# Graph attention over 400 000 edges: the row gathers of a pair of sections issued in four groups of two, four to five pairs ahead, in place of two groups of four, two to three pairs ahead

## The chip, the cores and the metric

The kernel runs on one core of a Trainium2 chip. The metric is the device time of one execution in microseconds (us), and smaller is better. Engines are named as in the profile: PE is TensorE (matrix products and transposes), DVE is VectorE, ACT is ScalarE, POOL is GpSimd, SP is SyncE. PEld is the loading of PE's weights, which overlaps its matmuls.

## The reference, cut to what matters

There are N = 12500 nodes with C = 128 channels and E = 400000 edges, sorted by target node. Each edge has 32 attributes and one weight; H = 8 heads.

```python
h = relu(layernorm(x))
msg_src, msg_dst = h @ w_src + b_src, h @ w_dst
rad = silu(silu(edge_attr_32 @ w1 + b1) @ w2 + b2) @ w3 + b3      # 32 -> 64 -> 64 -> 128
message = (msg_src[src] + msg_dst[dst]) * edge_weight1 * rad
message = message @ w_sep + b_sep                                 # 128 -> 256
alpha, value = per head, 16 + 16: smooth_leaky_relu(first), second
score = sum(alpha * alpha_dot)                                    # E x 8
att = softmax of score over the edges of one target node
out = x + segment_sum(value * att, dst) @ w_proj + b_proj
```

The row `msg_src[src]` is wanted for every edge, in a random order: these are the gathers of this case.

## The kernel before, in words

A first stage computes the two node tables `t_src` and `t_dst` in device memory (up to about 115 us in the profile). A last stage, from about 5610 us on, finishes the nodes. Between them stands `windows()`, nearly all of the time, and the change lies in it.

`windows()` works on pairs: a pair is 1000 edges, that is 2 sections of 500, and a section is 4 tiles of T = 125 edges. There are NP = 400 pairs. A function `step(k)` issues work for several pairs at once. The order of the instructions on each engine is the order in which `step` writes them down (the scheduler is switched off here); every engine runs its own list in order and waits for semaphores of the others. One step on PE, with the line of the profile in parentheses and c = k - 12:

1. `mlp3(k)` (L795): third layer of the radial network for pair k, 2 matmuls. Behind it DVE makes `rad` (L799), the layer's result plus bias, times the edge weights.
2. `sources(k,1)` (L808): 4 transposes of gathered rows of section 1 into the PSUM tile `pm1`.
3. `message(k)` (L816): 6 small matmuls that add the targets' rows through one-hot matrices. Behind it DVE makes `mT` (L821), that is (pm + bias) times `rad`, in two halves.
4. `values(c,0)` (L908): 4 matmuls for an older pair; DVE makes `pvx` (L910) of them.
5. `alphas(k,0)` (L825): needs the first half of mT. ACT makes `sl` (L827), DVE `al` (L829).
6. `mlp1(k+2)` (L763).
7. `values(c,1)` (L908), then on DVE `one_hot(c)` (L895, L898).
8. `sources(k+1,0)` (L808): 4 transposes of section 0 of the next pair into `pm0`.
9. `alphas(k,1)` (L825).
10. `mlp2(k+1)` (L778); ACT makes `h`, which the next step's mlp3 reads.
11. `sums(c)` (L919): 8 accumulating pairs of matmuls, copied out by ACT (`ob`, L923).
12. One step in eight: the transposes of the softmax (L880). Another one in eight makes indices for the gathers (`prep_make`, L697 and L700).
13. `e_T(k+3)` (L754): transposes of attributes; ACT copies them (`eT`, L756).
14. In odd steps: `scores(k)` (L836) for pairs k-1 and k; ACT copies them (`Sp`, L839).

The PSUM tiles have one buffer each, and together they fill its 8 banks: `p3` (two, shared by the three layers), `m1`, `pm0`, `pm1`, `pa`, `V` and `misc`, which is shared by sums, scores and the softmax.

The gathers (L744) are indirect DMAs issued by POOL: 128 rows of 512 bytes each, one per tile, so eight in a step. `gather(k,f)` fills a tile of 4 x 128 elements per partition, named gs0 or gs1, with two buffers of each name. It stands directly behind the `sources` call that frees the buffer it will fill, and POOL has nothing else to do in the steps: `gather(k+2,1)` waits for the transposes of `sources(k,1)`, `gather(k+3,0)` for those of `sources(k+1,0)`. POOL so issues two groups of four in each step.

The loads of attributes are issued by ACT, and the targets' rows (`md`, L724) are loaded four pairs ahead.

Of the kernel before, what the change touches and what calls it, by code (L numbers as in the profile page):

```python
# [21 lines left out]
F32 = mybir.dt.float32  # L22
# [8 lines left out]
P = 128  # L31
C = 128
# [13 lines left out]
T = 125  # L46
TS = 4
SEC = T * TS
# [8 lines left out]
def gnn_kernel(ctx: ExitStack, tc: tile.TileContext, a: dict, out: bass.AP):  # L57
    nc = tc.nc
# [46 lines left out]
    ident = const.tile([P, P], F32, name="ident")  # L105
# [22 lines left out]
    def zero(i):  # L128

        av = agg[0:N, :].rearrange("(p t) c -> p (t c)", p=RP)  # L130
        nc.sync.dma_start(out=av[:, i * zc * ROW:(i + 1) * zc * ROW], in_=z)
        if i == 0:
            nc.sync.dma_start(out=agg[N:N + W, :], in_=z[:W, 0:ROW])
# [527 lines left out]
    def windows():  # L661
# [5 lines left out]
        with tc.tile_pool(name="wk2", bufs=2) as sp, tc.tile_pool(name="ps", bufs=1, space=PSUM) as pp, \  # L667
                tc.manual_schedule(), ExitStack() as held:
            lp = held.enter_context(tc.tile_pool(name="ld", bufs=2))
            prep, e_g, d_g, w_g, md, gath = {}, {}, {}, {}, {}, {}  # L670
            eTs, h1s, h2s, ohT, m3, mr, mTs, als, S_all, sms, Ps, Pem, pvx, ohs, accs, xs, Ms, pms = (
                {} for _ in range(18))


            def prep_load(u):
                t0 = u * P
                ri = lp.tile([P, 2, T], I32, name="ri")
                rb = lp.tile([P, 1], I32, name="rb")
                nc.sync.dma_start(out=ri[:, 0, :], in_=src_t[t0:t0 + P, :])
                nc.sync.dma_start(out=ri[:, 1, :], in_=dst_t[t0:t0 + P, :])  # L680
                at = dst_t[t0:t0 + P, 0:1]
                (step, _), *_ = at.ap
                at = bass.AP(at.tensor, at.offset, [[step * TS, P // TS], [0, TS], [1, 1]])
                with nc.allow_non_contiguous_dma(reason="a word per tile"):
                    nc.sync.dma_start(out=rb, in_=at)
                prep[u] = (ri, rb)
# [22 lines left out]
            def load_d(g):  # L709
                d_g[g] = lp.tile([P, 2, SEC], I32, name="d_b")  # L710
                for f in range(2):
                    nc.sync.dma_start(
                        out=d_g[g][f * W:(f + 1) * W],
                        in_=dst_p[f:f + 1, 2 * g:2 * g + 2, :].to_broadcast([W, 2, SEC]))

            def load_w(k):
                w_g[k] = lp.tile([P, PR], F32, name="w_b", bufs=4)
                nc.sync.dma_start(out=w_g[k], in_=ew_p[:, k, :].to_broadcast([P, PR]))

            def load_md(k):  # L720
                md[k] = lp.tile([P, C], F32, name="md", bufs=5)
                at = [nc.sync.value_load(base[0:1, f, k:k + 1]) for f in range(2)]
                for f in range(2):
                    nc.sync.dma_start(out=md[k][f * W:(f + 1) * W, :], in_=t_dst[ds(at[f], W), :])  # L724
# [11 lines left out]
                else:  # L736
                    nc.vector.tensor_sub(m3[k][:, 2, :], mr.pop(k), m3[k][:, 1, :])

            def gather(k, f):
                gs = lp.tile([P, TS, C], F32, name=f"gs{f}", bufs=2)  # L740
                idx, _ = prep[k // 16]
                for j in range(TS):
                    t = k % 16 * 8 + f * TS + j
                    nc.gpsimd.indirect_dma_start(  # L744
                        out=gs[:, j, :], out_offset=None, in_=t_src[:, :],
                        in_offset=bass.IndirectOffsetOnAxis(ap=idx[:, t:t + 1], axis=0))
                gath[k, f] = gs


            def e_T(k):  # L750
# [49 lines left out]
                                                   op0=ALU.add, op1=ALU.mult)  # L800
                return rad

            def sources(k, f):

                gs = gath.pop((k, f))
                pms[k, f] = pp.tile([C, SEC], F32, name=f"pm{f}")
                for t in range(TS):
                    nc.tensor.matmul(pms[k, f][:, t * T:(t + 1) * T], gs[:T, t, :], ident[:T, :T],  # L808
                                     start=(t == 0), stop=False, is_transpose=True, skip_group_check=True)

            def message(k, rad):
# [11 lines left out]
            def alphas(k, f):  # L823
                pa = pp.tile([C, SEC], F32, name="pa")
                nc.tensor.matmul(pa, w_a, mTs[k][:, f * SEC:(f + 1) * SEC], start=True, stop=True)  # L825
                sl = sp.tile([C, SEC], F32, name="sl")
                nc.scalar.activation(sl, pa, AF.Silu, bias=b_a, scale=1.0)  # L827
                al = sp.tile([C, SEC], F32, name="al", bufs=6)
                nc.vector.scalar_tensor_tensor(al, pa, 0.25, sl, op0=ALU.mult, op1=ALU.add)  # L829
                als[2 * k + f] = al  # L830
# [46 lines left out]
            def softmax_T(m):  # L877
                pt = pp.tile([T, TS, P], F32, name="misc")
                for t in range(TS):
                    nc.tensor.transpose(pt[:, t, :], Ps[m][:, t * T:(t + 1) * T], ident)  # L880
                Pem[m] = sp.tile([T, TS, MQ, H], F32, name="Pem")
                nc.scalar.copy(Pem[m].rearrange("p t q h -> p t (q h)"), pt)
# [43 lines left out]
            def store_win(c):  # L926
                nc.sync.dma_start(out=win[c * P:(c + 1) * P, :], in_=accs[c])

            def store(c, f):
                at = nc.sync.value_load(base[0:1, f, c:c + 1])  # L930
                nc.sync.dma_start(out=agg[ds(at, W - 1), :], in_=accs[c][f * W:(f + 1) * W - 1, :])
# [16 lines left out]
            def has(k):  # L948
                return 0 <= k < NP
# [5 lines left out]
            def step(k):  # L955
                c = k - LAG
                if has(c - 1):
                    store_win(c - 1)
                    store(c - 1, 0)

                if k % 16 == 4 and has(k + 12):
                    prep_load((k + 12) // 16)
                if has(k + 3):
                    load_w(k + 3)
                if has(k + 4):
                    load_md(k + 4)
                if k % 2 and has(k + 3):
                    load_d((k + 3) // 2)
                if has(k + 4) and (k + 4) % MP == 0:
                    load_sm((k + 4) // MP)  # L970
                if has(c - 1):
                    store(c - 1, 1)
                if 0 <= 2 * k < NZ:
                    for i in range(2 * k, min(2 * k + 2, NZ)):
                        zero(i)
                if k % 16 == 8 and has(k + 8):
                    prep_make((k + 8) // 16)
                i, q = divmod(k - 40, MP)
                if 0 <= i < Q and q == 0:
                    load_x(i)  # L980
                if 0 <= i < Q and q == 7:
                    add_x(i)
                if has(k + 1):
                    split_md(k + 1, 0)
                if has(c):
                    weights(c)
                rad = mlp3(k) if has(k) else None
                if has(k):
                    sources(k, 1)
                if has(k + 2):  # L990
                    gather(k + 2, 1)
                if has(k):
                    message(k, rad)
                if has(c):
                    values(c, 0)
                if has(k + 1):
                    split_md(k + 1, 1)
                if has(k):
                    alphas(k, 0)
                if has(k + 6) and k >= -4:  # L1000
                    load_e(k + 6)
                if has(k + 1):
                    split_md(k + 1, 2)
                if has(k + 2):
                    mlp1(k + 2)
                if has(c):
                    values(c, 1)
                    one_hot(c)

                if has(k + 1):  # L1010
                    sources(k + 1, 0)
                if has(k + 3):
                    gather(k + 3, 0)
                if has(k):
                    alphas(k, 1)
                if has(k + 1):
                    mlp2(k + 1)
                    one_hot_T(k + 1)
                    split_md(k + 1, 3)
                if has(c):  # L1020
                    sums(c)
                m, r = divmod(k, MP)
                if has(k - MP):
                    if r == 1:
                        softmax_up(m - 1)
                    elif r == 2:
                        softmax_down(m - 1)
                        softmax_exp(m - 1)
                    elif r == 3:
                        softmax_T(m - 1)  # L1030
                if has(k + 3):
                    e_T(k + 3)
                if has(k) and k % 2 == 1:
                    scores(k)
# [187 lines left out]
    with tc.tile_pool(name="fin", bufs=3) as fp, tc.tile_pool(name="fin1", bufs=1) as f1, \  # L1222
# [7 lines left out]
        gs, qs, qTs, has = {}, {}, {}, {}  # L1230
# [104 lines left out]
```

## Time and profile before

| quantity | value |
|---|---|
| median of 3 runs (lowest, highest) | 5814.39 us (5809.36, 5816.74) |
| the profiled execution | 5814.39 us, its span 5812.6 us |
| mean granted clock of PE | 0.903 of full speed |
| mlp3 of the first and the last pair | 128 us and 5604 us, so 13.7 us a step |
| PE busy from 128 to 5603 us | 4402 us of 5475 us |
| POOL busy from 128 to 5603 us | 3105 us |
| a gather on POOL | 973 ns mean, 3200 of them |
| a transpose of gathered rows on PE | 300 ns mean, pipelined; 553.9 us busy in all |

How to read what follows: a group is all instructions of one line, engine and form; its columns are busy time, mean duration of one in ns, and idle time of its engine just before it with what ended that. A line of the waits says which engine and line waited for what, with the total in us, how often, and the longest. In the timeline each row has start, length, engine, line, and in brackets the idle time before it and its releaser. A window's row has its length, the busy time of PE, PEld, DVE, ACT and POOL with instructions, then the granted clock, the DMA engines' share and GB/s.

### The profile page before, as it was taken

To read this page: it belongs to the slowest core of one execution; us is meant where nothing else is said; L and a number is where in the kernel's file an instruction comes from. 1 tells how busy PE (TensorE), PEld (TensorE's weight loads), DVE (VectorE), ACT (ScalarE), POOL (GpSimd) and SP (SyncE) were. 2 spreads that over 40 slices of the span, in tenths; PEclk is the share of its full clock that TensorE was granted. 3 is DMA by queue.
4 is the path that set the end of the run, shared out by engine and by line. 5 is a ranking of instruction groups with operands and counts; after the bars stand their busy time and mean duration, and the time that the engine had idled before them with its cause. 6 is when DMAs were issued, how large, how long until landed. Compare 5 with 4: busy or idle time off the path is not lost.

```text
span 5812.6 us, 87691 instructions
## 1 busy us (share of the span) xinstructions
PE 4590.1 (79%) x29692; PEld 2537.5 (44%) x29692; DVE 3082.3 (53%) x6005; ACT 1903.7 (33%) x4595; POOL 3127.7 (54%) x3223
## 2 busy tenths in 40 slices
PE   5688788877788888888888888788888877788874
PEld 3244444444444444444444444444444444444444
DVE  5355555555555555555555555555555555555556
ACT  4233333333333333333333333333333333333321
POOL 1555555555555555555555555555555555555520
PEclk8898999989988989999899998998988999999987
DMA  6555555555555555555555555555555555555533
GB/s 200 162 138 129 136 139 137 141 132 141 136 132 135 144 131 138 146 134 136 143 133 140 143 130 133 139 132 130 137 129 135 139 127 128 133 134 133 137 82 144
DMA packets 901335, 794.74 MB, mean 137 GB/s; under 512 B 530270, under 2 KB 776974, under 8 KB 900746
## 3 DMA queue, kind: packets, MB, share of 16 engines
q1 hardware_dynamic: 394664, 520.94, 30.1%
q0 software_dynamic: 102816, 210.37, 17.1%
q10 hardware_dynamic: 403394, 57.74, 6.6%
q8 instruction: 234, 3.83, 0.3%
q14 instruction: 227, 1.86, 0.1%
HBM read 648.39 MB, written 140.67 MB: 136 GB/s over the span
## 4 chain that ended last, share of the span: by engine, by line
PE 70%; DVE 9%; issue 9%; another core or an unknown queue 6%; ACT 4%; DMA 2%; SPq 0%; ACTq 0%; DVEq 0%
PE pa L825 13%; PE V L908 13%; PE misc L919 8%; PE p L795 7%; PE pm L808 7%; PE pm L816 6%; PE p L763 4%; PE misc L836 4%; PE p L778 4%; PE m L754 3%; DVE mT L821 3%; DVE rad L799 2%; DVE pvx L910 1%; PE misc L880 1%
## 5 line engine op out<-in xcount | busy, mean ns | idle before, releaser
L744 POOL DMA_INDIRECT gs<-t_src,idx x3200 | 3113.2, 973 | 2470.6 <-PE pm L808 988.1
L827 ACT ACTIVATE sl<-pa,c_b_a 128x500 f32<-128x500 f32 x800 | 541.8, 677 | 2307.1 <-PE pa L825 1075.3
L825 PE MATMUL pa<-mT,c_w_a 128*128 128x500 f32 x1600 | 899.6, 646 | 389.4 <-DVE mT L821 305.1
L799 DVE SCALAR_TENSOR_TENSOR rad<-p,c_fc_b,w_b 128x500 f32<-128x500 f32 x800 | 553.4, 733 | 1145.9 <-PE p L795 541.4
L908 PE MATMUL V<-c_w_v,mT 128*125 128x128 f32 x6208 | 984.6, 307 | 125.0 <-DVE pvx L910 89.8
L908 PEld LDWEIGHTS V<-c_w_v,mT 128*125 128x125 f32 x6208 | 826.4, 207 | 441.8 <-issue 316.4
L910 DVE TENSOR_TENSOR pvx<-V,Pem 125x512 f32<-125x512 f32 x776 | 532.8, 687 | 680.6 <-PE pa L825 275.6
L829 DVE SCALAR_TENSOR_TENSOR al<-pa,sl 128x500 f32<-128x500 f32 x800 | 541.7, 677 | 553.8 <-ACT sl L827 335.7
L919 PE MATMUL misc<-pvx,oh 125*64 125x136 f32 x6400 | 486.4, 297 | 263.8 <-DVE oh L898 135.9
L821 DVE SCALAR_TENSOR_TENSOR mT<-pm,c_b_src,rad 128x500 f32<-128x500 f32 x800 | 554.3, 732 | 115.6 <-PE V L908 38.1
L919 PEld LDWEIGHTS misc<-pvx,oh 125*64 125x64 f32 x6400 | 380.9, 143 | 439.6 <-issue 278.0
L808 PE MATMUL pm<-ident,gs 125*128 125x125 f32 x3200 | 553.9, 300 | 3.3 <-DMA gs<-t_src,idx 2.4
L808 PEld LDWEIGHTS pm<-ident,gs 125*128 125x128 f32 x3200 | 400.4, 155 | 339.7 <-issue 335.1
L795 PE MATMUL p<-h,w3b 64*128 64x500 f32 x1600 | 487.6, 689 | 13.9 <-ACT h L781 7.7
L825 PEld LDWEIGHTS pa<-mT,c_w_a 128*128 128x128 f32 x1600 | 257.6, 202 | 455.8 <-DVE mT L821 350.5
L836 PE MATMUL misc<-al,w_s 128*32 128x500 f32 x1600 | 241.3, 669 | 168.8 <-issue 83.3
L923 ACT COPY ob<-misc 128x136 f32<-128x136 f32 x400 | 109.1, 273 | 707.8 <-PE m L754 400.7
L816 PE MATMUL pm<-ohT,m 64*128 64x500 bf16 x2400 | 338.6, 390 | 0.0
L763 PE MATMUL p<-eT,w1b 64*128 64x250 f32 x1600 | 307.9, 465 | 3.1 <-ACT eT L756 3.1
L778 PE MATMUL p<-h,w2b 64*64 64x250 f32 x3200 | 278.6, 420 | 26.1 <-ACT h L766 23.5
L766 ACT ACTIVATE h<-p,b 128x500 f32<-128x500 f32 x400 | 273.0, 683 | 38.3 <-issue 12.0
L781 ACT ACTIVATE h<-p,b 128x500 f32<-128x500 f32 x400 | 269.4, 673 | 30.6 <-remote 14.0
(145 smaller groups left out, 3274.6 us busy)
## 6 DMA issues: line engine op xcount, KB each, us to landing
w_b<-in_edge_weight SPq DMA_DIRECT2D x400, 500.0 KB
d_b<-in_dst SPq DMA_DIRECT2D x400, 250.0 KB
gs<-t_src,idx POOLq DMA_INDIRECT x3200
e_t<-in_edge_attr ACTq DMA_DIRECT2D x400, 125.0 KB
sc_d<-Sp SPq DMA_DIRECT2D x200, 250.0 KB
win<-ob SPq DMA_DIRECT2D x400, 68.0 KB
agg<-ob SPq DMA_DIRECT2D x800, 33.5 KB
md<-t_dst SPq DMA_DIRECT2D x800, 32.0 KB
```

The lines of the kernel that those rows point to most:

```text
L744: nc.gpsimd.indirect_dma_start(out=gs[:, j, :], out_offset=None, in_=t_src[:, :], in_offset=bass.IndirectOffsetOnAxis(ap=idx[:, t:t + 1], ...
L795: nc.tensor.matmul(p3[:, f, 0:SEC], w3b[s, :], h2s[k][s, :], start=True, stop=True)
L799: nc.vector.scalar_tensor_tensor(rad[:, s], p3[:, f, 0:SEC], b3, w_g[k][:, s], op0=ALU.add, op1=ALU.mult)
L808: nc.tensor.matmul(pms[k, f][:, t * T:(t + 1) * T], gs[:T, t, :], ident[:T, :T], start=(t == 0), stop=False, is_transpose=True, skip_group ...
L816: nc.tensor.matmul(pm[f], m3[k][s, j, :], ohT[k][s, :], start=False, stop=(j == 2), skip_group_check=True)
L821: nc.vector.scalar_tensor_tensor(mTs[k][:, s], pm[f], b_n, rad[:, s], op0=ALU.add, op1=ALU.mult)
L825: nc.tensor.matmul(pa, w_a, mTs[k][:, f * SEC:(f + 1) * SEC], start=True, stop=True)
L827: nc.scalar.activation(sl, pa, AF.Silu, bias=b_a, scale=1.0)
L829: nc.vector.scalar_tensor_tensor(al, pa, 0.25, sl, op0=ALU.mult, op1=ALU.add)
L908: nc.tensor.matmul(V[:, t, :], mTs[c][:, o:o + T], w_v, start=True, stop=True)
L910: nc.vector.tensor_mul(pvx[c][:, f, :, 0:C].rearrange("p t (h k) -> p t h k", h=H), V.rearrange("p t (h k) -> p t h k", h=H), Pem[c // MP] ...
L919: nc.tensor.matmul(acc[f * W:(f + 1) * W, :], ohs[c][:, f * TS + t, :], pvx[c][:, f, t, :], start=(t == 0), stop=(t == TS - 1), skip_group ...
```

## The change

The gathers of a section are split in two halves. `gather(k,f,h)` and `sources(k,f,h)` handle two tiles each; the tiles in SBUF become four names of 2 x 128 elements per partition with four buffers each, so that they take twice the room. Each gather still stands right behind the transposes that free its buffer, but fetches for four to five pairs ahead. The four groups of two transposes are put at four places of the step: behind mlp3, behind `values(c,1)`, behind `alphas(k,1)`, and ahead of `e_T`. So two of the transposes of section 1 that stood behind mlp3(k) are done at the end of step k-1. All other instructions of PE, and the lists of DVE, ACT and SP, keep their order; POOL's first gather of each of the four groups waits for PE.

The description of the change also names the loads of attributes by ACT and the rows of targets four pairs ahead; those are in the kernel before already, and the diff has only this:

```diff
-            def gather(k, f):
-                gs = lp.tile([P, TS, C], F32, name=f"gs{f}", bufs=2)
+            def gather(k, f, h):
+                gs = lp.tile([P, TS // 2, C], F32, name=f"gs{f}{h}", bufs=4)
                 idx, _ = prep[k // 16]
-                for j in range(TS):
-                    t = k % 16 * 8 + f * TS + j
+                for j in range(TS // 2):
+                    t = k % 16 * 8 + f * TS + h * 2 + j
                     nc.gpsimd.indirect_dma_start(
...
-                gath[k, f] = gs
+                gath[k, f, h] = gs
...
-            def sources(k, f):
-
-                gs = gath.pop((k, f))
-                pms[k, f] = pp.tile([C, SEC], F32, name=f"pm{f}")
-                for t in range(TS):
-                    nc.tensor.matmul(pms[k, f][:, t * T:(t + 1) * T], gs[:T, t, :], ident[:T, :T],
+            def sources(k, f, h):
+
+                gs = gath.pop((k, f, h))
+                if h == 0:
+                    pms[k, f] = pp.tile([C, SEC], F32, name=f"pm{f}")
+                for j in range(2):
+                    t = 2 * h + j
+                    nc.tensor.matmul(pms[k, f][:, t * T:(t + 1) * T], gs[:T, j, :], ident[:T, :T],
                                      start=(t == 0), stop=False, is_transpose=True, skip_group_check=True)
...
                 rad = mlp3(k) if has(k) else None
                 if has(k):
-                    sources(k, 1)
-                if has(k + 2):
-                    gather(k + 2, 1)
+                    sources(k, 1, 1)
+                if has(k + 4):
+                    gather(k + 4, 1, 1)
...
                 if has(k + 1):
-                    sources(k + 1, 0)
-                if has(k + 3):
-                    gather(k + 3, 0)
+                    sources(k + 1, 0, 0)
+                if has(k + 5):
+                    gather(k + 5, 0, 0)
                 if has(k):
                     alphas(k, 1)
+                if has(k + 1):
+                    sources(k + 1, 0, 1)
+                if has(k + 5):
+                    gather(k + 5, 0, 1)
                 if has(k + 1):
                     mlp2(k + 1)
...
+                if has(k + 1):
+                    sources(k + 1, 1, 0)
+                if has(k + 5):
+                    gather(k + 5, 1, 0)
                 if has(k + 3):
                     e_T(k + 3)
```

## The prediction

> **What bounds the kernel now.** I read the page first, then the groups of instructions, the waits, the windows of two steps and the timeline of the same two.
>
> From the page:
>
> ```profile
> PE 4590.1 (79%) x29692; PEld 2537.5 (44%) x29692; DVE 3082.3 (53%) x6005; ACT 1903.7 (33%) x4595; POOL 3127.7 (54%) x3223
> PE 70%; DVE 9%; issue 9%; another core or an unknown queue 6%; ACT 4%; DMA 2%; SPq 0%; ACTq 0%; DVEq 0%
> L744 POOL DMA_INDIRECT gs<-t_src,idx x3200 | 3113.2, 973 | 2470.6 <-PE pm L808 988.1
> L808 PE MATMUL pm<-ident,gs 125*128 125x125 f32 x3200 | 553.9, 300 | 3.3 <-DMA gs<-t_src,idx 2.4
> ```
>
> PE carries the end. The transposes wait 2.4 us for gathered rows in the whole run, so fetching rows earlier (the deeper look-ahead) can bring nothing by itself. POOL has room: eight gathers a step take about 10 us of a step of 13.7 us (the 400 steps stand between 128 and 5604 us).
>
> The waits of PE in the steps:
>
> ```profile
> PE pa L825 <- DVE mT L821: 305.1, 216, 4.7
> PE misc L919 <- DVE oh L898: 135.9, 94, 8.8
> PE misc L919 <- issue: 121.2, 128, 2.0
> PE misc L836 <- issue: 83.3, 66, 2.5
> PE misc L836 <- ACT ob L923: 66.4, 58, 5.3
> ```
>
> The first line is `alphas(k,0)` waiting for the DVE chain mlp3, rad, mT; the next two are `sums`. The windows of one odd and one even step (length first; ahead of the DMA share, the granted clock) show that the odd one is stalled and partly at a lower clock:
>
> ```profile
> 3002.40:3018.30 15.90, 12.21 (x78) 6.85 (x76) 8.69 (x17) 4.41 (x12) 10.51 (x11) 0.89 0.62 163
> 3018.30:3029.00 10.70, 9.42 (x72) 5.33 (x68) 7.01 (x14) 3.80 (x9) 6.33 (x7) 1.00 0.51 145
> ```
>
> Their timeline (start, length) says why:
>
> ```profile
> 3001.21 0.94 POOL L744 DMA_INDIRECT gs<-t_src,idx  x1 [1.29 <-PE p L778]
> 3002.49 1.11 PE L795 MATMUL p<-h,w3b 64*128 64x500 f32 x4
> 3004.95 0.95 POOL L744 DMA_INDIRECT gs<-t_src,idx  x1 [0.30 <-issue]
> 3005.60 1.38 DVE L799 SCALAR_TENSOR_TENSOR rad<-p,c_fc_b,w_b 128x500 f32<-128x500 f32 x2 [2.50 <-PE pm L816]
> 3008.01 1.10 PE L825 MATMUL pa<-mT,c_w_a 128*128 128x500 f32 x2 [2.02 <-DVE mT L821]
> 3010.09 2.07 PE L908 MATMUL V<-c_w_v,mT 128*125 128x128 f32 x8
> ...
> 3018.38 1.11 PE L795 MATMUL p<-h,w3b 64*128 64x500 f32 x4
> 3019.54 1.38 DVE L799 SCALAR_TENSOR_TENSOR rad<-p,c_fc_b,w_b 128x500 f32<-128x500 f32 x2 [2.65 <-PE p L795]
> 3021.71 1.03 PE L825 MATMUL pa<-mT,c_w_a 128*128 128x500 f32 x2
> ```
>
> In the even step rad starts 0.05 us after mlp3 has ended (3018.38 + 1.11 = 3019.49). In the odd one it starts 2.00 us after (3003.60 to 3005.60), though DVE idles 2.5 us and the rest of its data has long been there. Its start coincides with mlp3's semaphore update in the trace: PE had finished, its update came late. I set every PE update against the end of its matmul. They come 0.014 us after it, except while gathers run back to back. A run of four lasts 4.77 us; from 3.5 us after its start until about 1 us after its end, 9 of 10 updates are held, by 1.0 to 1.9 us (medians). In the 72 runs of eight, lags stay mostly under 1 us up to 5.2 us after the start, and are 2.7 to 3.4 us from 5.5 to 11.9 us. In the shown odd step the run of four began at 3001.21, so mlp3's end falls into its tail: rad is late, pa waits 2.02 us, and the next values matmuls run at half clock (2.07 us, where unstalled ones take 1.14). In even steps the other end of the same thing holds the update of `values(c,1)`: DVE's pvx and one_hot come late and `sums` waits. So the gathers' pattern in time sets about half of PE's idle time, though POOL is on no chain. That these held updates come from the gathers is read from their coincidence.
>
> The Trainium skill speaks against this reading: "SBUF — State Buffer", "Who interferes with whom", says that DMA traffic never contends with a compute engine and that PE waits for nobody's port. By it only the order on PE would count, and the sum would be +34 us; the rows above show the holds in this trace, whatever carries them.
>
> **The change part by part.** Sums are made against the profiled execution, 5814.39 us, the median of the three runs (span 5812.6, 1.8 around it).
>
> *Work.* Gathers, transposes and bytes stay 3200, 3200 and equal: 0. The buffers double in SBUF: 0. POOL waits for PE four times a step in place of two; what is queued behind each such wait are gathers only, and their rows are wanted four to five steps later: 0 as a wait.
>
> *Order on PE.* Two of the four transposes that stood between mlp3 and message go ahead of e_T and the next mlp3. Four take 0.58 us (mlp3's end to message's start less the 0.03 between), two 0.27 us net. At the end of an odd step they fill the wait of scores L836 (83.3 + 66.4 us over 200), and in the following even step pa was reached at +3.33 us, when mT's first half is done (0.05 + 1.11 + 1.38 + 0.73 = +3.27): 0. At the end of an even step nothing covers them, mlp3 starts 0.27 us later, and behind it the odd step is bound by the chain over rad: +0.27 x 200 = +54 us. `alphas(k,1)` moves ahead of two transposes: its results come 0.27 us sooner for scores, at most -54 us; I take -20, as scores' waits are 150 us and only some are for it.
>
> *When the gathers run.* Each group starts at the transposes that free its buffer. From the order and the durations of an unstalled step these are, from mlp3's start: 6.3 us (sources(k+1,0,0)), 7.3 (only alphas stands between), 9.2 (after sums), and the next step's, about 1.45 us after its mlp3. That is no quarter of a step each. One gather with its gap is 1.25 us, a group 2.5. Asked at 6.3, 7.3 and 9.2, three groups run back to back, 6.3 to 13.8; with steps of 10.7 to 13.7 us the fourth is asked for at 12.2 to 15.2, and follows with a gap of at most 1.4 us. So runs of six to eight, once a step, take the place of fours twice a step. By the rows of runs of eight, updates would be held from 5.5 us after the start, 11.8, to about 1 us after the end, 14.8 to 17.3: that is around mlp3 and message of the *next* step, in every step and not in every second.
> - Even steps: mlp3's update becomes late. Bounds: 0 (flushed just before) and 2.0 us as in odd steps; I take the middle, as the shown odd step is at the tail of its run and here the place is not sure to a microsecond: +1.0 x 200 = +200 us.
> - The lower clock behind such a wait: between 0 and 1.2 us (values 0.93, transposes 0.26); for a wait of half the size I take a quarter: +0.3 x 200 = +60.
> - Odd steps, held already: 2.0 us could become 2.7 to 3.4 (runs of eight), so 0 to +1.4; I take 0.5, the low side, as part lies behind the message's matmuls: +100.
> - `values(c,1)` ends at 6.2 us, ahead of the run: its hold goes. Bounds 0 and the whole of the two waits of sums, -257 us; I take -150, as pvx then waits for the later mT and al on DVE.
>
> Sum: 54 - 20 + 200 + 60 + 100 - 150 = +244 us, **6058 us**. What is late next is rad in every step. The terms' ends give -311 (0 for the order and the late updates, -54, -257) and +974 (54 + 400 + 240 + 280), so 5503 to 6788.
>
> **Rivals.**
> 1. *Faster: short bursts are not held.* In the runs of four the first two gathers mostly see no lag (median 0.02 to 0.04 us), and after a pause of more than 2.2 us the count begins anew. If the groups really come apart, by stalls that spread their triggers, the holds go: pa's 305 and sums' 257 us, and about 150 us of lower clock, 712 in all. That decides from a pause of some 1.4 us after each group on. Against it: the triggers at 6.3 and 7.3 stand 1.0 us apart in any step. Half of it, 356 us, gives 5458.
> 2. *Only the order counts:* the holds neither grow nor shrink, as both patterns keep POOL busy equally long. +34, 5848 us, slower. For it: POOL's 3113 us do not change.
> 3. *The full hold in every step:* 2.0 us and the clock in even steps, 1.4 more in odd ones, nothing back from sums beyond half: 974 - 128 = +846, 6660 us. For it: the 2.7 to 3.4 us of runs of eight. Against it: a stalled step is longer, so the run ends earlier in the next one and frees mlp3's update again.
>
> The change failing to do what it says (a quarter of a step apart) is in the forecast itself.
>
> **How the numbers follow.** Forecast 0.45, rival 1 0.27, rival 2 0.13, rival 3 0.15. A measurement of this kernel tells about 0.2%, 12 us, from no change. Rival 1 is faster, a small part of the forecast's low side as well: 0.28; within 0.2%: 0.04; slower 0.68. The forecast's own range is 5800 to 6350. For 8 in 10 it reaches down into rival 1, to 5480, and up into rival 3, to 6500.
>
> **What would show it.** Right: in the timeline, POOL runs of six or more gathers a step; rad starting 1 us and more after mlp3's end in even steps too; pa's wait for mT well over 305 us in twice as many instances; sums' waits below 257. Wrong: gathers in pairs with gaps over a microsecond, pa's wait falling below 150 us and a granted clock over 0.93 (rival 1); or the same waits as now with runs of another length (rival 2), which would say that the pattern of the gathers does not make the holds. DMA waits of the transposes above some 20 us would refute that the rows arrive in time.

## The result and the profile after

The changed kernel takes 6163.97 us (median of 4 runs, 6146.42 to 6174.31), the kernel before 5811.88 us beside it. The ratio is 1.0604 with a 95% interval of 1.0574 to 1.0634, so the change costs 352 us; 244 were forecast. The profiled execution took 6146.42 us, its span is 6144.6 us and the mean granted clock 0.882 (before: 5812.6 and 0.903).

The page of the changed kernel; the lines of the transposes and of `alphas` have moved by two, L808 to L810 and L825 to L827:

```profile
PE 4741.6 (77%) x29692; PEld 2635.2 (43%) x29692; DVE 3095.0 (50%) x6005; ACT 1952.1 (32%) x4595; POOL 3133.6 (51%) x3223
PE 71%; DVE 9%; issue 9%; another core or an unknown queue 7%; ACT 2%; DMA 2%; SPq 0%; POOL 0%; ACTq 0%; POOLq 0%; DVEq 0%
L744 POOL DMA_INDIRECT gs<-t_src,idx x3200 | 3119.1, 975 | 2775.2 <-PE pm L810 1480.3
L810 PE MATMUL pm<-ident,gs 125*128 125x125 f32 x3200 | 705.3, 305 | 6.9 <-DMA gs<-t_src,idx 5.1
```

PE still carries the end, the transposes still wait for almost no row (5.1 us), and POOL is as busy as before; only its waits for the transposes' updates grew, from 988 to 1480 us. The groups of `alphas` and `sums` (last figure before the arrow: idle time of PE ahead of them) show where the time went:

```profile
L827 PE MATMUL pa<-mT,c_w_a 128*128 128x500 f32 x1600 | 1004.5, 714 | 756.3 <-DVE mT L823 410.6 <-issue 165.1 <-DVE rad L799 148.4
L921 PE MATMUL misc<-pvx,oh 125*64 125x136 f32 x6400 | 468.9, 289 | 96.1 <-DVE oh L900 54.3 <-issue 38.1 <-DVE pvx L912 1.6
```

Before, these two idle times were 389.4 and 263.8 us. So PE waits 367 us longer ahead of `alphas` and 168 us less ahead of `sums`. PE's busy time grew by 151 us (4590.1 to 4741.6) for the same instructions: that is the lower clock, as the time at half clock grew from 1126 to 1447 us and costs half of itself. 367 - 168 + 151 = 350 us, against 332 us of span.

Rows of the timeline of an even step of the changed kernel (others left out); the first is the first gather of a run of six, the third the last:

```profile
3253.46 0.94 POOL L744 DMA_INDIRECT gs<-t_src,idx  x1 [2.15 <-PE pm L810]
3259.02 1.11 PE L795 MATMUL p<-h,w3b 64*128 64x500 f32 x4
3259.72 0.94 POOL L744 DMA_INDIRECT gs<-t_src,idx  x1 [0.30 <-issue]
3262.07 1.38 DVE L799 SCALAR_TENSOR_TENSOR rad<-p,c_fc_b,w_b 128x500 f32<-128x500 f32 x2 [5.97 <-PE pm L818]
3264.16 1.10 PE L827 MATMUL pa<-mT,c_w_a 128*128 128x500 f32 x2 [1.85 <-DVE mT L823]
3265.82 2.06 PE L910 MATMUL V<-c_w_v,mT 128*125 128x128 f32 x8
```

mlp3 ends at 3260.13, rad starts at 3262.07, though DVE has idled 5.97 us: the late update that only odd steps had before. `alphas` waits 1.85 us, and the next values matmuls run at half clock. Not every even step is like this one: in pairs 48 to 383, rad starts 1 us or more after mlp3's end in 36% of the even steps (4% before) and in 85% of the odd ones (53% before), and in over half of the even steps less than 0.3 us after it (median 0.05).

A late or held update means, below, that the semaphore update by which PE tells others that a matmul is done comes long after the matmul's end. In some measurements the kernel before takes 4467 to 4482 us and hardly an update of PE is late, in others 5798 to 5874 us, as above, with late updates; every comparison below is between kernels that were measured together.

### The profile page after: what moved, and what is told of

It is laid out like the page before. It is cut to its first block, busy times and chain, and to the rows that moved or that the text cites. A ratio compares the mean times of both kernels' runs of the same rounds, so it can differ in the third digit from the quotient of the medians.

```text
span 6144.6 us, 88478 instructions
## 1 busy us (share of the span) xinstructions
PE 4741.6 (77%) x29692; PEld 2635.2 (43%) x29692; DVE 3095.0 (50%) x6005; ACT 1952.1 (32%) x4595; POOL 3133.6 (51%) x3223
## 4 chain that ended last, share of the span: by engine, by line
PE 71%; DVE 9%; issue 9%; another core or an unknown queue 7%; ACT 2%; DMA 2%; SPq 0%; POOL 0%; ACTq 0%; POOLq 0%; DVEq 0%
PE pa L827 14%; PE V L910 14%; PE pm L810 8%; PE p L795 7%; PE misc L921 7%; PE pm L818 7%; PE p L763 5%; PE misc L838 4%; PE p L778 4%; DVE rad L799 4%; DVE mT L823 2%; PE m L754 2%; DVE pvx L912 1%; PE misc L882 0%
## 5 line engine op out<-in xcount | busy, mean ns | idle before, releaser
L827 PE MATMUL pa<-mT,c_w_a 128*128 128x500 f32 x1600 | 1004.5, 714 | 756.3 <-DVE mT L823 410.6
L910 PE MATMUL V<-c_w_v,mT 128*125 128x128 f32 x6208 | 1040.2, 318 | 126.1 <-DVE pvx L912 112.8
L910 PEld LDWEIGHTS V<-c_w_v,mT 128*125 128x125 f32 x6208 | 876.7, 218 | 464.2 <-issue 273.9
L810 PE MATMUL pm<-ident,gs 125*128 125x125 f32 x3200 | 705.3, 305 | 6.9 <-DMA gs<-t_src,idx 5.1
L810 PEld LDWEIGHTS pm<-ident,gs 125*128 125x128 f32 x3200 | 420.5, 155 | 658.5 <-issue 650.4
L827 PEld LDWEIGHTS pa<-mT,c_w_a 128*128 128x128 f32 x1600 | 288.5, 225 | 839.8 <-DVE mT L823 445.2
L921 PE MATMUL misc<-pvx,oh 125*64 125x136 f32 x6400 | 468.9, 289 | 96.1 <-DVE oh L900 54.3
L795 PE MATMUL p<-h,w3b 64*128 64x500 f32 x1600 | 483.3, 683 | 7.5 <-ACT h L781 4.9
L921 PEld LDWEIGHTS misc<-pvx,oh 125*64 125x64 f32 x6400 | 366.1, 139 | 260.3 <-issue 185.9
L838 PE MATMUL misc<-al,w_s 128*32 128x500 f32 x1600 | 232.7, 649 | 168.5 <-issue 85.7
L763 PE MATMUL p<-eT,w1b 64*128 64x250 f32 x1600 | 339.8, 508 | 2.2 <-ACT eT L756 2.2
L763 PEld LDWEIGHTS p<-eT,w1b 64*128 64x128 f32 x1600 | 143.8, 220 | 362.7 <-issue 356.0
```

The costliest lines, as they stand in the source:

```text
L763: nc.tensor.matmul(p1[:, q, 0:2 * T], w1b[s, :], eTs[k][s, :], start=True, stop=True)
L795: nc.tensor.matmul(p3[:, f, 0:SEC], w3b[s, :], h2s[k][s, :], start=True, stop=True)
L810: nc.tensor.matmul(pms[k, f][:, t * T:(t + 1) * T], gs[:T, j, :], ident[:T, :T], start=(t == 0), stop=False, is_transpose=True, skip_group ...
L910: nc.tensor.matmul(V[:, t, :], mTs[c][:, o:o + T], w_v, start=True, stop=True)
L921: nc.tensor.matmul(acc[f * W:(f + 1) * W, :], ohs[c][:, f * TS + t, :], pvx[c][:, f, t, :], start=(t == 0), stop=(t == TS - 1), skip_group ...
```

## Experiments where no update is held

The first four kernels were measured beside a kernel before of 4481.70 us.

**Order alone.** PE's order of the changed kernel, gathers in two fours, tiles and look-ahead of the kernel before (parts of the edit, against the changed kernel):

```diff
                 if has(k):
                     sources(k, 1, 1)
-                if has(k + 4):
-                    gather(k + 4, 1, 1)
+                if has(k + 2):
+                    gather(k + 2, 1)
...
                     sources(k + 1, 0, 0)
-                if has(k + 5):
-                    gather(k + 5, 0, 0)
...
                     sources(k + 1, 0, 1)
-                if has(k + 5):
-                    gather(k + 5, 0, 1)
+                if has(k + 3):
+                    gather(k + 3, 0)
...
                     sources(k + 1, 1, 0)
-                if has(k + 5):
-                    gather(k + 5, 1, 0)
```

> PE's order of the changed kernel (transposes in four groups of two), gathers in two groups of four as before, each behind the transposes that free its tile. Theory (the pattern of the gathers in time makes the loss through held PE updates): only the order counts, +34 us, about 5850 us (5800 to 5900), PE's wait at alphas near 0.9 us a step as before. Rival (the moved transposes make the loss, since the cover before alphas is gone): about 6160 us, alphas' wait near 1.8 us a step.

Measured: 4525.43 us, ratio 1.0104 (1.0087 to 1.0121), +43.7 us.

**Gathers alone.** PE's order of before; behind `sources(k+1,0)` its four gathers and, on buffers that are free already, two of section 1 (against the changed kernel):

```diff
-                if has(k + 1):
-                    sources(k + 1, 1, 0)
-                if has(k + 5):
-                    gather(k + 5, 1, 0)
+                if has(k + 4):
+                    gather(k + 4, 1, 0)
```

with both halves of `sources(k,1)` behind mlp3 and both of `sources(k+1,0)` ahead of `alphas(k,1)`.

> The other way round: PE's order of before (four transposes behind mlp3, four behind values), but six gathers in a row from sources(k+1,0) on and two behind sources(k,1), tiles and depth of the changed kernel. Theory: the loss is here, 6100 to 6250 us, alphas' wait 1.5 to 2.0 us a step, sums' wait well under the 0.59 us of before. Rival (order): about 5815 us, waits as before.

Measured: 4488.95 us, 1.0018 (1.0008 to 1.0028).

**Each split alone.** In the first, section 1 is put back (against the changed kernel):

```diff
+                for h in range(2):
+                    if has(k):
+                        sources(k, 1, h)
+                    if has(k + 4):
+                        gather(k + 4, 1, h)
...
-                if has(k + 1):
-                    sources(k + 1, 1, 0)
-                if has(k + 5):
-                    gather(k + 5, 1, 0)
```

> The changed kernel with section 1 put back (four transposes and four gathers behind mlp3); only section 0 is split around alphas(k,1), and all gathers are four to five pairs ahead. Theory: the two halves of section 0 are asked for 1.0 us apart and run back to back as before, so about 5815 us (5780 to 5860). Rival (each split costs its share, or the depth does): about 5990 us.

Measured: 4483.01 us, 1.0002 (0.9992 to 1.0011). In the second, section 0 is put back in the same way, its two halves and their gathers ahead of `alphas(k,1)`.

> The changed kernel with section 0 put back (four transposes and four gathers behind values); only section 1 is split, its first half at the end of the step before. Theory: the group at the end of the step lengthens the run of four into one of six and makes nearly the whole loss, 6100 to 6200 us. Rival (each split costs its share): about 5990 us.

Measured: 4534.07 us, 1.0118 (1.0101 to 1.0135).

The times expected were for a kernel of 5812 us, and did not come. The profile of the first split shows a different picture for the same instructions (page; the third line is the granted clock in 40 slices):

```profile
PE 4151.2 (93%) x29692; PEld 2343.8 (52%) x29692; DVE 3092.6 (69%) x6005; ACT 1956.6 (44%) x4595; POOL 3111.4 (69%) x3223
PE   6689999999999999999999999999999999999964
PEclk9789999999999999999999999999999999999987
```

PE's updates come 0.014 us after the modelled ends in the median, in all four kernels, though the gathers run back to back here, in runs of up to 128 (gathers alone). So back-to-back gathers alone do not hold updates; something that is not in the program has to be there too. What these runs do settle is the price of the order without holds: it is the split of section 1 (1.0118; the split of section 0 and the depth of four to five pairs cost nothing, 1.0002). It is no wait: PE idles 0.14 us a step ahead of `alphas` (pairs 48 to 383) in the order and gathers kernels alike, and PE is busy 48 us longer (4203.3 against 4154.9 us).

The changed kernel itself was measured next, to see its price without held updates:

> The changed kernel itself, beside the kernel before on the chip of this call; the four runs so far, on a chip where the kernel before takes 4482 us and no update of PE is held, do not hold it. If the chip again shows no held updates (lag of PE's updates near 0.02 us, no lower clock), theory (the order costs some 45 us, the rest of the loss is held updates): the sum of the order's and the gathers' parts there, about 4535 us against 4482, ratio 1.010 to 1.014. Rival (the change costs the same share everywhere): ratio 1.06. If the chip holds updates as in the first profile, the ratio is 1.06 under both and nothing is told apart.

It met late updates again: 6255.05 us against 5846.57, 1.0702 (1.0635 to 1.0770), so a second measure of the result and nothing told apart. Three kernels made for a place with late updates came next, and met none:

> PE's order of the changed kernel, gathers in two fours as before (same kernel as the first run of this name), now for a chip that holds PE's updates, where the kernel before takes about 5810 to 5850 us. Theory (the rest of the loss is made by the moved gathers): the order's part alone, +44 us as on the chip without holds, at most +120 with more lower clock, so 5860 to 5960, with the held share of mlp3's updates as before. Rival (the moved transposes make the loss on such a chip, since the shorter cover meets the late rad): 6160 to 6260. On a chip without holds: +44 us again.

> PE's order of before, six gathers in a row from sources(k+1,0) on and two behind sources(k,1), for a chip that holds PE's updates. Theory: +200 to +320 us on the kernel before, alphas' wait 1.5 to 2.0 us a step. Rival (order): within 1% of the kernel before. On a chip without holds: +8 us again.

> The kernel before with the indirect gathers by POOL replaced by plain DMAs of as many bytes from SP's queue (512 consecutive rows a section instead of the edges' rows, so the computation is not the reference's); POOL is idle in the steps. Theory (POOL's gathers hold PE's updates): no updates held, no lower clock, 4480 to 4600 us even on a chip where the kernel before takes 5810 to 5850. Rival (the holds come from PE's own load or from the DMA traffic, which stays): 5600 us and more there. On a chip without holds: about 4480 us, which tells nothing.

Measured, against 4467.11 us: order 4513.73 (1.0095, 1.0077 to 1.0113), gathers 4470.58 (1.0006, 0.9997 to 1.0016), and the third, whose edit is

```diff
-                idx, _ = prep[k // 16]
-                for j in range(TS):
-                    t = k % 16 * 8 + f * TS + j
-                    nc.gpsimd.indirect_dma_start(
...
+                r0 = (2 * k + f) * TS * P % (N - TS * P)
+                nc.sync.dma_start(out=gs, in_=t_src[r0:r0 + TS * P, :].rearrange("(j p) c -> p j c", p=P))
```

4488.91 (1.0051, 1.0035 to 1.0068). Where no update is held, taking POOL's gathers away wins nothing.

## Experiments where updates are held: stages in one kernel

Since separate kernels could meet late updates or not, I put the patterns into one kernel as stages of the run: `variant(k)` gives the pattern of a step by its pair, and each place of the step asks for it.

```diff
+            def variant(k):
+                at = 0
+                for name, cycles in PLAN:
+                    at += cycles * MP
+                    if k < at:
+                        return name
...
                 if has(k + 1):
                     sources(k + 1, 0, 0)
+                    if not late:
+                        sources(k + 1, 0, 1)
+                if v != "order":
+                    fetch(0, 0, k + 5)
...
+                if late and has(k + 1):
                     sources(k + 1, 1, 0)
+                if v == "after":
+                    fetch(1, 0, k + 5)
+                elif v == "gathers":
+                    fetch(1, 0, k + 4 if has(k + 4) else NP)
```

`fetch` issues what is missing of a tile's gathers up to a pair; `late` is true in the stages after and order.

> One kernel whose steps change their pattern every few cycles of eight pairs, so that all patterns meet the same chip in one execution (all with the changed kernel's tiles, four to five pairs ahead): fours (as before), after (the changed kernel), order (its transposes, gathers in fours), gathers (transposes as before, six gathers in a row and two), these four twice for four cycles each; then sp (plain DMAs of consecutive rows from SP in place of the gathers, POOL idle) and half (one gather per tile of two in place of two, so two runs of two a step), which leave out the edges' own rows, and fours again. To be read as the mean step of each stage without its first cycle. On a chip that holds PE's updates, theory (the gathers' pattern makes the holds): fours 13.7 us, order 13.9, gathers 14.3 to 14.6, after 14.5, sp 10.3 (as on a chip without holds), half 10.5 to 12. Rival 1 (PE's order makes the loss there): order 14.5, gathers 13.7. Rival 2 (the holds are not made by the gathers): sp and half 13.7. On a chip without holds: fours, gathers, sp and half 10.3, order and after 10.4 to 10.45.

The first execution met no late updates (before 4467.08 us): 10.29 to 10.30 us a step for fours, gathers 10.29, sp 10.27, half 10.26, order 10.41, after 10.41 and 10.48.

> The kernel of stages once more, hoping for a chip that holds PE's updates. Expected there as before: theory (the gathers' pattern makes the holds) fours 13.7 us a step, order 13.9, gathers 14.3 to 14.6, after 14.5, sp 10.3, half 10.5 to 12; rival 1 (order) order 14.5, gathers 13.7; rival 2 (not the gathers) sp and half 13.7. On a chip without holds: as in the first run, 10.3 for fours, gathers, sp and half, 10.4 to 10.5 for after and order.

The second did (before 5798.36 us). The windows of its stages, without the first cycle of each; 24 steps each, 32 in the last two. First comes the length, ahead of the last two figures the granted clock. In order: fours, after, order, gathers, the same again, then sp and half.

```profile
597.30:933.20 335.90, 267.08 (x1750) 143.79 (x1746) 174.88 (x333) 110.23 (x268) 187.50 (x192) 0.91 0.54 134
1048.70:1392.70 344.00, 274.64 (x1748) 152.87 (x1744) 175.21 (x334) 112.68 (x268) 187.29 (x194) 0.90 0.52 132
1498.50:1829.00 330.50, 262.87 (x1750) 146.22 (x1746) 173.93 (x334) 111.72 (x269) 184.89 (x193) 0.93 0.55 138
1947.50:2312.40 364.90, 282.24 (x1748) 153.75 (x1744) 176.12 (x334) 110.73 (x268) 188.25 (x195) 0.87 0.50 125
2428.20:2767.50 339.30, 267.55 (x1750) 144.50 (x1746) 175.00 (x334) 110.21 (x268) 187.72 (x192) 0.90 0.55 134
2881.10:3232.30 351.20, 279.65 (x1750) 154.30 (x1746) 175.75 (x334) 112.95 (x268) 187.35 (x192) 0.88 0.51 129
3343.70:3672.70 329.00, 260.10 (x1748) 144.16 (x1745) 173.01 (x334) 111.49 (x268) 185.00 (x193) 0.94 0.55 136
3797.50:4172.40 374.90, 287.11 (x1748) 157.33 (x1744) 174.80 (x331) 111.20 (x268) 185.19 (x191) 0.85 0.46 117
4253.90:4583.50 329.60, 318.89 (x2328) 175.79 (x2324) 230.23 (x440) 147.47 (x352) 1.89 (x2) 1.00 0.71 176
4667.50:5006.10 338.60, 319.90 (x2326) 176.03 (x2325) 230.25 (x440) 143.75 (x352) 124.48 (x130) 0.99 0.61 148
```

Per step: fours 14.00 and 14.14, after 14.33 and 14.63, order 13.77 and 13.71, gathers 15.20 and 15.62, sp 10.30, half 10.58 us. The closing fours took 13.58 us in the three whole cycles behind their first. In sp POOL is all but idle (1.89 us), PE is at full clock and busy 97% of the time, with more DMA traffic per us (176 GB/s against 134): the step is that of the runs without holds. So POOL's gathers carry the holds, and neither PE's load nor the amount of DMA traffic does. What it is in a gather, POOL's issuing, its queue or the random rows, sp does not tell: it takes all three away.

The two rivals fall. The order alone costs nothing that can be told here: 13.74 us against 13.90 for the three stages of fours, whose cycles lie between 13.49 and 14.31. The gathers' pattern alone costs 1.5 us a step (15.41). The changed kernel, with both, costs 0.6 here (14.48) and 0.8 between the first two traces (13.72 and 14.51, pairs 48 to 383). The steps go with the gathers' runs, that is with how many follow each other with less than 0.5 us between them: of the gathers, 15% stand in runs longer than four in order, 19% in fours, 43% in after and 80% in gathers. That the changed kernel costs less than its gathers' pattern alone, I had not foreseen; its groups come apart more often.

Runs of two, twice a step, are nearly free: in half, rad starts 0.14 us after mlp3's end on the mean, as in sp, against 0.78 in fours. But half has also half the gathers, so length and number of the gathers are not told apart by it.

The third kernel of stages asked whether another pacing of all eight gathers escapes the holds, and whether more cover behind mlp3 does. Its new pieces:

```diff
+                if paced:
+                    nc.vector.memset(gs[0:1, j, 0:1], 0.0)
                 nc.gpsimd.indirect_dma_start(
...
+                if v[:4] == "slow":
+                    nc.gpsimd.memset(idle[:, 0:int(v[4:])], 0.0)
...
+                if v == "early":
+                    if has(k + 1):
+                        rads[k + 1] = mlp3(k + 1)
+                    if has(c):
+                        sums(c)
```

> Again a kernel of stages, all in PE's order of the kernel before and with the tiles of the changed one; to be read as the mean step of each stage without its first cycle. fours: as before. slow128 and slow16: fours with a memset of POOL behind each gather (128 or 16 elements a partition, about 0.2 and 0.1 us), so that gathers cannot follow each other closer than about 1.5 and 1.4 us. singles: each gather waits for one of eight places of DVE's list spread over the step (a one-element write to its tile there), quarters: two gathers at each of four places about a quarter of a step apart. early: fours, with mlp3 of the next pair and its rad ahead of sums, so that a late update of mlp3 has some 1.5 us more cover. On a chip that holds PE's updates: theory (what is held stands behind a backlog of the gathers, which drains at about 1.45 us a gather: runs of four are clear 5.75 us after their start, runs of eight 11.9) gives slow128 12.0 to 12.6, slow16 11.5 to 13, singles 12 to 13, quarters 12.5 to 13.8, early 12.5 to 13.3, fours 13.7 to 14. Rival (any run longer than three gathers holds, however slow): slow128 14 and more, slow16 and singles as fours. On a chip without holds: slow128 12.0 to 12.3 and slow16 11.0 to 11.4, bound by POOL, the others 10.2 to 10.4.

It met late updates (before 5808.30 us). The windows, in the order fours (24 steps), slow128, slow16 (48 each), singles, quarters, early (56 each):

```profile
594.20:923.10 328.90, 260.81 (x1748) 144.00 (x1744) 174.35 (x333) 109.85 (x269) 186.40 (x193) 0.93 0.55 137
1046.30:1719.30 673.00, 535.17 (x3492) 288.06 (x3488) 352.90 (x666) 218.06 (x528) 457.35 (x765) 0.90 0.54 135
1834.90:2495.40 660.50, 525.62 (x3489) 288.24 (x3488) 351.45 (x666) 217.87 (x528) 425.29 (x768) 0.92 0.55 137
2607.40:3447.30 839.90, 661.98 (x4072) 348.38 (x4068) 415.14 (x1226) 253.45 (x620) 443.92 (x449) 0.85 0.50 126
3563.00:4374.00 811.00, 639.25 (x4072) 344.34 (x4068) 414.76 (x1219) 256.18 (x620) 433.27 (x449) 0.89 0.51 126
4485.50:5217.50 732.00, 609.48 (x4067) 323.75 (x4066) 408.15 (x767) 249.89 (x616) 429.32 (x448) 0.96 0.58 139
```

Per step: fours 13.70 (the closing ones, in three whole cycles, 13.93), slow128 14.02, slow16 13.76, singles 15.00, quarters 14.48, early 13.07 us. The pauses did not space the gathers as intended, because a gather leaves POOL idle for 0.30 us anyway, and the memset goes into that time (slow128):

```profile
1406.05 0.23 POOL L754 MEMSET idle<- 128x128 f32 x1
1406.44 0.95 POOL L750 DMA_INDIRECT gs<-t_src,idx  x1 [0.17 <-issue]
```

The gathers of a run start 1.34 us apart in slow128 and 1.26 us in slow16 (medians), against 1.25 us without memsets, not 1.5 and 1.4. So the gain that I expected did not come, but a backlog that drains at 1.45 us a gather is not refuted by this: in neither stage were the gathers of a run that far apart. Nor are the gathers of singles and quarters evenly spaced: 60% and 34% of them stand in runs longer than four, and 8% and 1% alone. (These two stages also add a write by DVE, and a wait for it, to each gather.) What eight gathers a step would cost if they really stood apart was not measured. What the stages add is the same ranking: 18% of the gathers in longer runs for fours and slow16, 34 to 35% for slow128 and quarters, 60% for singles. Only more cover behind mlp3 gained, so I ran that edit alone on the kernel before:

```diff
-                rad = mlp3(k) if has(k) else None
+                rad = (rads.pop(k) if k in rads else mlp3(k)) if has(k) else None
...
-                if has(c):
-                    sums(c)
...
                     scores(k)
+                if has(k + 1):
+                    rads[k + 1] = mlp3(k + 1)
+                if has(c):
+                    sums(c)
```

> The kernel before with mlp3 of the next pair (and its rad on DVE) put at the end of the step, ahead of sums, and nothing else: gathers in two fours, tiles and depth of before. On a chip that holds PE's updates, theory (what costs is that the held update is mlp3's, with no cover on the way to alphas): as the stage early showed, 0.65 to 0.85 us a step less, 5480 to 5560 us against about 5810, ratio 0.94 to 0.96. Rival (that stage was faster by its place in the run or by its tiles alone): ratio 0.99 to 1.01. On a chip without holds: alphas' wait of 0.14 us a step is all that can go, ratio 0.985 to 1.00.

Measured: 5759.40 us against 5873.66, ratio 0.9806 (0.9754 to 0.9858). It beats both kernels where updates are held, but by 1.9% and not by the 4 to 6% expected. PE's waits show why less came than was removed (the kernel before in its first trace):

```profile
PE pa L825 <- DVE mT L821: 222.5, 156, 11.5
PE V L908 <- DVE pvx L910: 152.7, 71, 4.4
PE p L795 <- ACT h L781: 134.9, 47, 7.0
PE p L795 <- ACT sl L827: 104.9, 89, 1.8
PE p L795 <- issue: 97.5, 87, 3.4
PE misc L919 <- DVE oh L898: 33.3, 12, 8.6
```

Alphas' wait for mT fell from 305 to 222 us and sums' for the one-hot rows from 136 to 33, but mlp3 itself, closer now to the layer that feeds it, waits 337 us (the three lines of L795; 14 us before), a good part of it for ACT's h. The wait moved up the chain. Why the stage gained 5% and the whole kernel less (its tiles are those of before, with two buffers) stays open, as does its time where nothing is held, which was not measured.

## Why the prediction was right

**The direction and size** (244 forecast, 352 measured, within the range). By its own terms, on the first trace of each kernel:

| term | forecast | measured |
|---|---|---|
| rad later, even steps | +1.0 us a step | +0.78 |
| rad later, odd steps | +0.5 us a step | +0.49 |
| PE's wait ahead of alphas (200 + 100 + 54) | +354 us | +367 (389.4 to 756.3) |
| PE's wait ahead of scores | -20 us | 0 (168.8 to 168.5) |
| PE's wait ahead of sums | -150 us | -168 (263.8 to 96.1) |
| lower clock | +60 us | +151 (PE busy), +160 (half of 321 us more at half clock) |

The means of rad's lateness are over pairs 48 to 383, by place in the cycle of eight. The mis-sized term is the clock: I took a quarter of what follows a full wait, for half a wait in every even step. What came are long waits in about a third of the even steps and none in most, and the timeline above shows the full slowing (V at 2.06 us) after a wait of 1.85 us. With 151 for 60 the sum is 335. That 354 stands so near 367 is in part luck: the measured lateness of rad makes 0.78 x 200 + 0.49 x 200 = 254 us, and the 54 us for the order are not seen where updates are held.

Of the signs that I named, runs of six and more came and sums' waits fell. The waits of pa (for mT, rad and issue together) came 313 times in place of 249, not twice as often, and rad is not late in most even steps.

The Trainium skill ("TensorE: Matmul & The Clock Gate", Part 1) puts the fall to half rate behind an idle window of about 3.4 us; here waits of 1.85 and 2.02 us have slow matmuls behind them, so less idle time is enough. In the trace of before, the granted clock is half from 3009.18 to 3012.59; in the 3.41 us ahead of that PE was busy for 1.39 us. The windows of the stages give a clock of 0.85 to 0.96 where updates are held, 0.99 in half and 1.00 in sp.

**The mechanism: shown in part.** That POOL's gathers carry the late updates is shown by sp; that longer runs of them cost more, by the gathers stage, and the ranking of the other stages agrees. In the changed kernel (pairs 48 to 383) rad starts 2.7 us after mlp3 on the mean when mlp3 ends within a run of six (85 steps), 1.8 us within a run of four (105), 0.6 us within a run of eight, where it ends early in the run (68), and 0.06 us behind a run of two (49). So runs of six made most of the rise, where I had reckoned with six to eight in every step. That mlp3's late updates alone make the loss is argued from PE's waits: in singles rad is only 0.23 us late on the mean, and the step still takes 15.00 us. The page "SBUF — State Buffer" of the Trainium skill (Who interferes with whom), as the prediction read it, agrees with the runs without holds (updates 0.014 us late with gathers back to back) and not with the others (10.30 us a step without POOL's gathers, 13.6 to 14.1 with them).

**The steps that failed.** First, "runs of six to eight, once a step, take the place of fours twice a step". In pairs 48 to 383 there are 217 runs of two, 265 of four, 96 of six and 68 of eight; 43% of the gathers stand in runs longer than four (18% before). The second group does follow the first without a pause, in 99% of the steps, but the one at the step's end does so in 51% and the one behind mlp3 in 54%. I took the triggers from an unstalled step; they are PE's updates too, and those of the transposes at the end of the step come 1.3 us late on the mean, and POOL's wait for the transposes rose from 988 to 1480 us. Second, the rule that a hold begins so and so long after a run's start. It does not apply at all where updates are not held, and whether a backlog that drains lies behind it stays open. Two readings of it were off as well: in the odd step shown, mlp3 ends 2.4 us after the run's start (3003.60 and 3001.21), which is not the tail of the run, and ahead of the 3.5 us of the rule; and set against the first update recorded behind each matmul's end, the lags in runs of eight have medians (over half microseconds) of 1.0 to 2.7 us between 5.5 and 11 us, not 2.7 to 3.4.

**The order:** +34 forecast. Without holds it costs +44 and +47 us, but as PE's own time and not as the uncovered wait that I priced; with holds it costs nothing that the stages can tell (13.74 against 13.90 us a step). The number was near for the wrong reason.

**Rivals.** The faster one claimed that short bursts are not held: true for two runs of two a step (10.58), which are also half the gathers, and open for all eight, as quarters (14.48) did not keep them apart. Its full price of 712 us was far too low: without holds a step is 3.3 to 3.8 us shorter, 1300 to 1400 us between the kernels, as I had counted two of PE's waits and 150 us of clock, where fours lose 2.9 us of idle time a step (sp: 0.33) and have 2.6 us at half clock (sp: none). Rival 2, order only, is what happens where updates are not held.

## What to carry to other kernels

Before a stall is put down to an engine's end, look at when its semaphore update came: an engine can be done for 2 us while its consumer idles. When separate runs cannot be compared, put the variants into one kernel as stages, so that one execution compares them. Look in the trace whether an edit that is to space work out did so, before its time is read: here the pauses went into idle time that was there already. Work whose own waits are all hidden (2.4 and 5.1 us here) can still lose time by what it delays when it runs in longer bursts.

## What was not expected of the hardware

The same kernel takes 4467 to 4482 us in three measurements and 5798 to 5874 us in five, with the same instructions, bytes and order. In the first the gathers run back to back and PE's updates are 0.014 us late in the median; in the others about half of the updates are over 0.3 us late, and PE waits and slows down. The gathers are needed for it (sp), but they do not suffice. What else is needed the runs do not show: the number that a result gives for its chip, 14, stands once beside 4467 us and once beside 5874 us.

A caution on all lags of updates: where they are late, some have no record of their own (7537 records for 8570 instructions of PE that update, in the trace of before; 8396 for 8563 in the first split), and the next one recorded is taken. The starts of rad do not depend on that.
